# A four-layer convolution kernel: x1's last count in two parts, the last norm's factors in two parts, steps of giving out moved among x3's factors, three buffers for the normed columns

## The chip, the core and the metric

The kernel runs on one core of a Trainium2 chip. The metric is the device time of one execution in microseconds, and lower is better. A core has five engines that each work through their own queue of instructions: PE (TensorE, matrix products), DVE (VectorE), ACT (ScalarE), POOL (GpSimd) and SP (SyncE, which here only issues transfers). "PEld" is PE's loading of weights.

## What is computed

Four layers follow each other, each added to its input after a group norm over groups of four channels. The tensor has 4 images of 128 x 128 places with 128 channels.

```
x = x + relu(deform_conv(gn(x)))          # layer 0, bilinear samples at learned offsets
x = x + scan(gn(x), W)                    # layer 1, row y uses row y-1 through a 9-tap conv
x = x + z_self + z_m + z_k                # layer 2, sums over rows and columns
x = x + triangle(gn(x))                   # layer 3:
    xn = layer_norm(x); left, right = xn@left_w * sigmoid(..), xn@right_w * sigmoid(..)
    out = einsum('bkjd,bkid->bijd', left, right)
    out = (layer_norm(out) * out_gate) @ to_out_w
```

`gn` needs the mean and the variance of a whole image before any of it can be normed; in the last layer the layer norm of `out` needs them for each of its columns of 128 channels.

## The kernel before

All engines run in the order in which the program emits their instructions (`tc.manual_schedule`); generators with `yield` interleave the streams by hand, and a `step(...)` advances one of them.

**Layer 0** (`deform_layer`, lines 189 to 774) goes through blocks of three rows. Finished rows go into chunks of 16 rows (`x1c`, L576), are stored to DRAM (L586), and DVE counts each chunk, group by group (`bn_stats`, L590), into `stats`, which holds 8 chunks. When an image is done, `gn_steps` (L153) aggregates the eight counts of each of 32 groups (`bn_aggr`, L158), averages over partitions with two small matmuls (L165, L177) and ends in `scale_shift` (L92 to L96). For the last image this happens after the last convolution (L755 to L760). Then `far` is worked out: whether an offset was over 1 (L764 to L773). All engines load `far`, and jump over a general form of the layer where it is 0 (L1725).

**Layer 1** (`scan_layer`, L1011) loads rows of x1 (L1055), turns them (L1064), norms them on ACT (L1068) and runs the recurrence (L1101 to L1142), with PE nearly always busy.

**Layers 2 and 3** (`last_layers`, L1286) go image by image (L1663 to L1701). For an image b: `messages` (L1338) makes layer 2's result and counts it; `scaled` (L1389) turns the counts into factors of x3 (aggregation L1393, small matmuls L1396, L1407, L1419, square root L1409, reciprocal L1410); `normed` (L1463) centres and norms in 25 steps; `multiplied` (L1513) makes left, right and their products in four quarters of 24 steps. Between them, one step at a time, runs `given_out(b - 1)` (L1563), which norms the products of the image before, gates, multiplies by `to_out_w`, adds x3 and stores. The last image's giving out runs alone at the end (L1702); the code calls that `alone`.

One giving out has 40 steps, k from -7 to 32. Step k stores block k-1 (L1604), loads x3 for block k+2 (L1607), turns the normed columns of block k+1 on PE (L1612), makes y on ACT (L1614) and gates it (L1615, on POOL, or on DVE if alone), multiplies block k (L1623, L1627), counts block k+7 (L1578), norms the columns of block k+2 into `u` (ACT L1642, POOL L1640), evicts block k (L1644) and loads gates (L1649). In every fourth step `scales` (L1580) makes the factors for a group of four blocks from their counts: four small DVE operations (L1589 to L1592), a square root on ACT (L1595), a reciprocal and a product on DVE (L1596, L1597). They are first used by `u` two steps later. `u` has two buffers. ACT needs another table for the square root than for the sigmoids of `multiplied`, and loads it in between.

Of the kernel before, what the change touches and what calls it, by code (L numbers as in the profile page):

```python
# [10 lines left out]
F32 = mybir.dt.float32  # L11
# [3 lines left out]
ALU = mybir.AluOpType  # L15
# [4 lines left out]
P = 128  # L20
B = 4
S = 128
# [4 lines left out]
GS = 4  # L27
NGN = P // GS
# [121 lines left out]
    return (mean, *scale_shift(nc, c, keep, mean, var, tag))  # L150


def gn_steps(nc, c, work, keep, psum, stats, tag, got):  # L153

    n = stats.shape[2]
    mv = work.tile([P, NGN, 2], F32, name="gf_mv")
    for g in range(NGN):
        nc.vector.bn_aggr(mv[:, g, :], stats[:, g, :, :].rearrange("p n s -> p (n s)", n=n))  # L158
        if g % 8 == 7:
            yield  # L160
    mean_bc = psum.tile([P, NGN], F32, name="gn_ps", tag="gn_ps")
    mcol = work.tile([P, NGN], F32, name="gf_mcol")
    nc.vector.tensor_copy(mcol, mv[:, :, 0])
    yield
    nc.tensor.matmul(mean_bc, lhsT=c.mean, rhs=mcol, start=True, stop=True)  # L165
    yield
    d = work.tile([P, NGN], F32, name="gf_d")
    nc.vector.tensor_tensor(d, mcol, mean_bc, ALU.subtract)
    nc.vector.tensor_tensor(d, d, d, ALU.mult)
    nc.vector.tensor_tensor(d, d, mv[:, :, 1], ALU.add)  # L170
    wide = work.tile([P, 2, NGN, GS], F32, name="gf_wide")
    nc.vector.tensor_copy(wide[:, 0], mcol.unsqueeze(2).to_broadcast([P, NGN, GS]))
    nc.vector.tensor_copy(wide[:, 1], d.unsqueeze(2).to_broadcast([P, NGN, GS]))
    yield
    col = psum.tile([P, 2], F32, name="gn_ps2", tag="gn_ps")
    for i in range(2):
        nc.tensor.matmul(  # L177
            col[:, i : i + 1], lhsT=wide[:, i].rearrange("p g r -> p (g r)"),
            rhs=c.mean[:, 0:1], start=True, stop=True,
        )  # L180
    yield
    mvp = work.tile([P, 2], F32, name="gf_mvp")
    nc.vector.tensor_copy(mvp, col)
    yield
    got.extend(scale_shift(nc, c, keep, mvp[:, 0:1], mvp[:, 1:2], tag))
    yield


def deform_layer(tc, c, small, x, w_off, b_off, w_def, x1, tabs, offs):
# [11 lines left out]
    nc = tc.nc  # L201
# [6 lines left out]
    with ExitStack() as ctx:  # L208
        wp = ctx.enter_context(tc.tile_pool(name="l0w", bufs=1))
        keep = ctx.enter_context(tc.tile_pool(name="l0keep", bufs=2))  # L210
        one = ctx.enter_context(tc.tile_pool(name="l0one", bufs=1))
        two = ctx.enter_context(tc.tile_pool(name="l0two", bufs=2))
        three = ctx.enter_context(tc.tile_pool(name="l0three", bufs=3))
# [73 lines left out]
        last = moving("parts_of_last", 2, 1)  # L287
# [300 lines left out]
        def count(n):  # L588
            for _ in range(min(n, len(to_count))):
                nc.vector.bn_stats(*to_count.pop(0))  # L590
# [40 lines left out]
        ready = [0] * B  # L631
        beside = {"now": None, "norms": [], "rows": 0, "count": iter(())}

        def x1_norm(b, stats):
            got = []
            yield from gn_steps(nc, c, one, small, ps_g, stats, f"x1_{b}", got)
            norms[b] = got[1:]

        def counting(b):
# [74 lines left out]
        for n, (b, j) in enumerate(blocks):  # L714
# [29 lines left out]
            else:  # L744
# [7 lines left out]
                        stats, NU // 2,  # L752
                    ),
                )
        for _ in convs:  # L755
            pass
        count(len(to_count))
        beside["norms"].append(x1_norm(B - 1, stats))
        while step():
            pass  # L760

# [9 lines left out]
        nc.vector.tensor_scalar(row, row, 1.0, None, ALU.is_gt)  # L771
        far = small.tile([1, 1], I32, name="far")
        nc.vector.tensor_copy(far, row)  # L773
        return norms, far


# [509 lines left out]
def last_layers(tc, c, terms, w, x2T, out, x3T, gateT, stdT):  # L1286
# [9 lines left out]
    with ExitStack() as ctx:  # L1296
# [20 lines left out]
        def single(shape=(P, 512)):  # L1317
            return ps_s.tile(list(shape), F32, name="one_ps", tag="one_ps")
# [70 lines left out]
        def scaled(b):  # L1389

            stats = xs.pop(b)
            mv = two.tile([P, 2], F32, name="mv3")
            nc.vector.bn_aggr(mv, stats.rearrange("p n s -> p (n s)"))  # L1393
            nc.vector.tensor_tensor(mv[:, 0:1], mv[:, 0:1], w.outb, ALU.subtract)
            mean_ps = single((P, 1))
            nc.tensor.matmul(mean_ps, lhsT=c.gmean, rhs=mv[:, 0:1], start=True, stop=True)  # L1396
            mean = two.tile([P, 1], F32, name="mean3")
            nc.vector.tensor_copy(mean, mean_ps)
            d = two.tile([P, 1], F32, name="d3")
            nc.vector.tensor_tensor(d, mv[:, 0:1], mean, ALU.subtract)  # L1400
            nc.vector.tensor_tensor(d, d, d, ALU.mult)
            nc.vector.tensor_tensor(d, d, mv[:, 1:2], ALU.add)
            for j0 in range(S // 2 if b else 0, S, 16):
                nc.scalar.dma_start(x3T[b, :, j0 : j0 + 16, :], X[:, j0 : j0 + 16, :])
            yield
            var_ps = single((P, 1))
            nc.tensor.matmul(var_ps, lhsT=c.gmean, rhs=d, start=True, stop=True)  # L1407
            s = two.tile([P, 1], F32, name="s3")
            nc.scalar.activation(s, var_ps, AF.Sqrt, bias=c.eps)  # L1409
            nc.vector.reciprocal(s, s)  # L1410
            cs = one.tile([P, P], F32, name="cs")
            nc.vector.tensor_scalar(cs, c.center, s, None, ALU.mult)

            shift = two.tile([P, 1], F32, name="shift")
            nc.vector.tensor_tensor(shift, mean, w.outb, ALU.add)
            nc.vector.scalar_tensor_tensor(shift, shift, -1.0, s, ALU.mult, ALU.mult)
            yield
            pc = single((P, 1))
            nc.tensor.matmul(pc, lhsT=c.center, rhs=shift, start=True, stop=True)  # L1419
            ct = two.tile([P, 1], F32, name="ct")  # L1420
            nc.vector.tensor_copy(ct, pc)
            to_one = two.tile([P, 1], F32, name="to_one")
            nc.vector.tensor_copy(to_one, ct)
            nc.vector.memset(to_one[0:1], 1.0)
            xs[b] = cs, ct, to_one
            yield
# [136 lines left out]
        def given_out(b):  # L1563
# [6 lines left out]
            if alone:  # L1570
                groups.update({1: 0, 4: 1})
            st, factors, us, ys, gates, x3s, outs = {}, {}, {}, {}, {}, {}, {}

            def statistics(k):
                if k % 4 == 0:
# [4 lines left out]
            def scales(k0, k1):  # L1580

                n = 4 * (k1 - k0)
                both = two.tile([P, n, 2], F32, name="both", tag=f"both{n}")
                apart = two.tile([P, n], F32, name="apart", tag=f"apart{n}")
                rs = two.tile([P, n], F32, name="rs", tag=f"rs{n}")
                nm = two.tile([P, n], F32, name="nm", tag=f"nm{n}")

                s = st[k0 // 4][:, k0 % 4 * 4 : k0 % 4 * 4 + n]
                nc.vector.tensor_tensor(both, s[:, :, 1:3], s[:, :, 4:6], ALU.add)  # L1589
                nc.vector.tensor_tensor(apart, s[:, :, 1], s[:, :, 4], ALU.subtract)  # L1590
                nc.vector.tensor_tensor(apart, apart, apart, ALU.mult)
                nc.vector.scalar_tensor_tensor(  # L1592
                    rs, apart, P / 4.0, both[:, :, 1], ALU.mult, ALU.add
                )
                nc.scalar.activation(rs, rs, AF.Sqrt, bias=c.eps, scale=1.0 / P)  # L1595
                nc.vector.reciprocal(rs, rs)  # L1596
                nc.vector.scalar_tensor_tensor(nm, both[:, :, 0], -0.5, rs, ALU.mult, ALU.mult)  # L1597
                for k in range(k0, k1):
                    at = [slice(i, i + 1) for i in range(4 * (k - k0), 4 * (k - k0) + 4)]
                    factors[k] = [(rs[:, i], nm[:, i]) for i in at]  # L1600

            for k in range(-7, NS_ + 1):
                if 0 <= k - 1:
# [25 lines left out]
                        )  # L1629
                if k + 7 < NS_:  # L1630
                    statistics(k + 7)
                    if k + 8 in groups:
                        scales(groups[k + 8], k + 8)
                if 0 <= k + 2 < NS_:
                    u = us[k + 2] = two.tile([P, 4, P], F32, name="u")
                    for j, (r, m) in enumerate(factors.pop(k + 2)):
                        of = column(b, 4 * (k + 2) + j)
                        to = u[:, j].rearrange("p (q d) -> p q d", q=NQ)
                        if j >= (1 if alone else 2):
                            nc.gpsimd.tensor_scalar(to, of, r, m, ALU.mult, ALU.add)  # L1640
                        else:
                            nc.scalar.activation(to, of, AF.Identity, bias=m, scale=r)  # L1642
                if 0 <= k < NS_:
                    nc.scalar.copy(x3, po)  # L1644
                    outs[k] = x3
                k += 3 if alone else 2
                if 0 <= k < NS_:
                    gates[k] = three.tile([P, 4, S], F32, name="gate")
# [8 lines left out]
        def step(of, n=1):  # L1657
            return all([next(of, END) is not END for _ in range(n)])
# [4 lines left out]
        for b in range(B):  # L1663

            for n, _ in enumerate(msgs):
                if n % 2:
                    step(out_of)
            for _ in scaled(b):
                pass
            norm = normed(b)  # L1670
            for n in range(25):
                step(norm)
# [114 lines left out]
```

## Time and profile before

| what | value |
|---|---|
| time, median of 3 runs | 5434.85 us (5428.95 to 5440.65) |
| the profiled execution's own time | 5449.07 us |
| its span, first to last instruction | 5447.3 us |
| mean granted clock of PE | 0.957 |

| stretch (us) | what runs | PE busy (us) | DVE busy (us) | ACT busy (us) | PE clock |
|---|---|---|---|---|---|
| 0 to 3050 | layer 0 | 2752.57 | 1844.85 | 1463.35 | 0.96 |
| 3050 to 3068 | its last convolution | 17.35 | 0.92 | 0.00 | 0.69 |
| 3068 to 3098 | x1's last norm, the jump, first rows | 2.25 | 16.92 | 0.29 | 0.50 |
| 3098 to 3958 | scan | 853.32 | 582.34 | 259.90 | 0.99 |
| 4027 to 4311 | layer 3, image 0 | 248.97 | 167.36 | 100.22 | 0.96 |
| 4311 to 4666 | image 1, image 0 given out | 312.13 | 214.08 | 181.08 | 0.95 |
| 4666 to 5020 | image 2, image 1 given out | 309.98 | 213.74 | 181.28 | 0.96 |
| 5020 to 5329 | image 3, image 2 given out | 280.62 | 161.33 | 180.91 | 0.96 |
| 5329 to 5448 | image 3 given out, alone | 81.47 | 74.94 | 62.27 | 0.77 |

In lines of a group or of the timeline, "out<-in" names the tiles; what stands in brackets or after the bar is the engine's idle time just before, and what ended it. A line of the waits says who waited for whom, in total, how often, and the longest.

### The profile page before, as it was taken

To read this page: it belongs to the slowest core of one execution; us is meant where nothing else is said; L and a number is where in the kernel's file an instruction comes from. 1 tells how busy PE (TensorE), PEld (TensorE's weight loads), DVE (VectorE), ACT (ScalarE), POOL (GpSimd) and SP (SyncE) were. 2 spreads that over 40 slices of the span, in tenths; PEclk is the share of its full clock that TensorE was granted. 3 is DMA by queue.
4 is the path that set the end of the run, shared out by engine and by line. 5 is a ranking of instruction groups with operands and counts; after the bars stand their busy time and mean duration, and the time that the engine had idled before them with its cause. 6 is when DMAs were issued, how large, how long until landed. Compare 5 with 4: busy or idle time off the path is not lost. (4 is left out here: it accounts for less than half of the span.)

```text
span 5447.3 us, 162742 instructions
## 1 busy us (share of the span) xinstructions
PE 4898.7 (90%) x68902; PEld 4254.0 (78%) x68902; DVE 3333.0 (61%) x8447; ACT 2431.9 (45%) x5045; POOL 1233.1 (23%) x1145
## 2 busy tenths in 40 slices
PE   1898999999999898989999799999969889798897
PEld 1787788888888787877899799999928578485686
DVE  4676666666566666665555466666664765756645
ACT  1554454544554444545544223333324364463655
POOL 4222121210221201212100011111120342422424
PEclk9999999999998999999999899999989999999997
DMA  5776656675666665665644322222242554645535
GB/s 151 160 159 150 138 135 141 147 151 102 137 142 132 150 121 110 147 132 119 132 83 89 85 82 78 78 78 78 67 142 92 174 182 130 212 144 170 187 113 194
DMA packets 1357657, 710.41 MB, mean 130 GB/s; under 512 B 943885, under 2 KB 1210414, under 8 KB 1347702
## 3 DMA queue, kind: packets, MB, share of 16 engines
q1 hardware_dynamic: 1322770, 624.74, 47.0%
q10 hardware_dynamic: 34148, 75.15, 3.7%
q8 instruction: 545, 8.93, 0.7%
q14 instruction: 194, 1.59, 0.1%
HBM read 417.02 MB, written 282.55 MB: 128 GB/s over the span
## 5 line engine op out<-in xcount | busy, mean ns | idle before, releaser
L606 PE MATMUL conv_ps<-ring,wdef 128*128 128x192 f32 (+2 forms) x7632 | 1301.6, 320 | 7.1 <-DVE x1c L576 5.7
L514 DVE TENSOR_TENSOR m<-t_ps,tent 128x390 f32<-128x390 f32 x1548 | 806.2, 557 | 788.7 <-ACT tent L512 772.8
L606 PEld LDWEIGHTS conv_ps<-ring,wdef 128*128 128x128 f32 x7632 | 1147.6, 196 | 127.6 <-issue 64.0
L512 ACT COPY tent<-t_ps 128x390 f32<-128x390 f32 x1560 | 691.1, 488 | 659.7 <-PE t_ps L498 648.3
L498 PE MATMUL t_ps<-parts_of,spread 57*64 57x99 bf16 (+1 forms) x12384 | 743.6, 275 | 168.1 <-DVE m L514 146.4
L523 PE MATMUL v_ps<-m,pixels 60*64 60x108 f32 (+1 forms) x22704 | 813.4, 264 | 20.3 <-DVE m L514 8.7
L498 PEld LDWEIGHTS <-spread 57*64 57x64 bf16 x12480 | 579.3, 126 | 312.1 <-issue 265.1
L523 PEld LDWEIGHTS v_ps<-m,pixels 60*64 60x64 f32 x22704 | 673.5, 137 | 70.5 <-DVE m L514 21.7
L549 ACT COPY ring<-v_ps 128x432 f32<-128x432 f32 x1032 | 505.7, 525 | 445.3 <-PE v_ps L523 444.7
L1526 PEld LDWEIGHTS pair_ps<-wcat,X 128*128 128x128 f32 x4096 | 491.0, 196 | 118.3 <-issue 75.3
L420 POOL TENSOR_TENSOR off<-off,koff 72x512 f32<-72x512 f32 x128 | 162.8, 1272 | 1772.7 <-DVE off L417 1772.7
L1526 PE MATMUL pair_ps<-wcat,X 128*128 128x128 f32 x4096 | 505.4, 281 | 57.4 <-DVE X L1461 36.1
L1534 DVE TENSOR_TENSOR T<-pair_ps,sig 128x256 f32<-128x256 f32 x512 | 281.4, 592 | 366.0 <-ACT sig L1531 365.4
L1112 PEld LDWEIGHTS own_ps<-diff,wconv 128*128 128x128 f32 x4064 | 494.8, 191 | 13.3
L1112 PE MATMUL own_ps<-diff,wconv 128*128 128x128 f32 x4064 | 495.6, 273 | 0.0
L506 PE MATMUL t_ps<-parts_of,spread 57*64 57x130 bf16 x9288 | 455.5, 225 | 0.0
L1152 POOL TENSOR_TENSOR sum_h<-sum_h,x2c 128x512 f32<-128x512 f32 x128 | 163.2, 1275 | 1147.3 <-DVE x2c L1138 689.8
L438 DVE SCALAR_TENSOR_TENSOR parts<-off,parts 72x512 bf16<-72x512 f32 x384 | 296.3, 772 | 152.2 <-ACT parts L430 146.5
L1068 ACT ACTIVATE rowT<-x1T_ps,t_x,s_x 128x128 f32<-128x128 f32 x512 | 207.2, 567 | 310.2 <-PE x1T_ps L1064 307.6
L506 PEld LDWEIGHTS <-spread 57*64 57x64 bf16 x9312 | 320.0, 108 | 0.1
L1531 ACT ACTIVATE sig<-pair_ps 128x512 f32<-128x512 f32 x256 | 152.4, 597 | 365.0 <-PE pair_ps L1526 264.3
L1101 PE MATMUL both_ps<-carry,wsum 128*128 128x128 f32 x2032 | 269.2, 274 | 1.1 <-DVE carry L1135 1.1
(200 smaller groups left out, 6681.0 us busy)
## 6 DMA issues: line engine op xcount, KB each, us to landing
pixels<-tab SPq DMA_DIRECT2D x688, 123.8 KB
parts_of<-off SPq DMA_DIRECT2D x1032, 55.7 KB
off<-parts SPq DMA_DIRECT2D x64, 891.0 KB
tab<-rows SPq DMA_DIRECT2D x384, 128.0 KB
xin<-in_x_dram SPq DMA_DIRECT2D x128, 256.0 KB
x<-x1c SPq DMA_DIRECT2D x32, 1024.0 KB
x1rows<-x SPq DMA_DIRECT2D x128, 256.0 KB
x2T<-x2c ACTq DMA_DIRECT2D x128, 256.0 KB
```

The costliest lines, as they stand in the source:

```text
L438: nc.vector.scalar_tensor_tensor(parts[:, NSPLIT + i, h : h + RO, 2 : S + 2], off, 0.0, part, ALU.is_gt, ALU.mult,)
L498: nc.tensor.matmul(tp[h : h + HALF, 0, 0:n].rearrange("p (r c) -> p r c", c=PADW)[:, :, i:PADW:RX], lhsT=spread[0:k, kx // 2, i, h : h + H ...
L506: nc.tensor.matmul(tp[h : h + HALF, 1, i * PADW : (i + 1) * PADW], lhsT=spread[HALF : HALF + k, kx // 2, first + i, h : h + HALF], rhs=src ...
L512: nc.scalar.copy(tent[:, 0:n], tp[:, 0, 0:n])
L514: nc.vector.tensor_tensor(m, *pair, ALU.mult)
L523: nc.tensor.matmul(to[p1 : p1 + HALF], lhsT=pix[p0 : p0 + LANES, xb, :], rhs=m[p0 : p0 + LANES, :, RX * xb : RX * xb + w], start=True, sto ...
L549: nc.scalar.copy(to, bodies[side])
L606: nc.tensor.matmul(pc[:, at : at + rows, x0:x1], lhsT=wdef[:, side, k, :], rhs=v[:, :, k if v.shape[2] == NK else kx, x0 + kx : x1 + kx], ...
L1101: nc.tensor.matmul(both, lhsT=wsum[:, j, :], rhs=old[h][:, 1, :, j : j + V], start=(j == 0), stop=(j == NJ - 1),)
L1112: nc.tensor.matmul(own[:, n], lhsT=wt[:, 2 * j + n, :], rhs=diffs[h][:, n, :, j : j + V], start=False, stop=(n == 1 and j == NJ - 1),)
L1526: nc.tensor.matmul(pj[:, j], lhsT=X[:, j0 + j, :], rhs=w.wcat[:, q * 4 * DQ : (q + 1) * 4 * DQ], start=True, stop=True,)
L1534: nc.vector.tensor_tensor(to, pj[:, :, e].rearrange("p j d -> p d j"), sig[:, :, e].rearrange("p j d -> p d j"), ALU.mult,)
```

## The change

Four edits:

1. `gn_steps` takes `apart`. With it, it aggregates only the first 7 of 8 counts of each group, and joins the eighth by ten operations on 128 x 32 (128 x 64) elements. For the last image, 8 of the 32 aggregations are emitted after each of four parts of the last convolution, then the last chunk is counted and joined. `far` is worked out before that convolution.
2. `scales` is a generator in three parts: DVE's four operations in the step in which it was, the square root, the reciprocal and the product at the end of the next step. The factors are so made one step later, and used in the step after.
3. `u` has three buffers.
4. `scaled` has one more `yield`, after L1394, and at its first two yields a step of giving out is made. There are no more steps than before: each step from the third on comes two places earlier, and the last two places, in the last quarter of `multiplied`, are empty.

```diff
-def gn_steps(nc, c, work, keep, psum, stats, tag, got):
+def gn_steps(nc, c, work, keep, psum, stats, tag, got, apart=False):
-    n = stats.shape[2]
+    n = stats.shape[2] - apart
     mv = work.tile([P, NGN, 2], F32, name="gf_mv")
     for g in range(NGN):
-        nc.vector.bn_aggr(mv[:, g, :], stats[:, g, :, :].rearrange("p n s -> p (n s)", n=n))
+        nc.vector.bn_aggr(mv[:, g, :], stats[:, g, 0:n, :].rearrange("p n s -> p (n s)", n=n))
         if g % 8 == 7:
             yield
+    if apart:
+        h, last = S // (n + 1) * GS / 2.0, stats[:, :, n, :]
+        both = work.tile([P, NGN, 2], F32, name="gf_both")
+        off = work.tile([P, NGN], F32, name="gf_off")
+        nc.vector.tensor_tensor(both, last[:, :, 1:3], last[:, :, 4:6], ALU.add)
+        nc.vector.tensor_tensor(off, last[:, :, 1], last[:, :, 4], ALU.subtract)
+        nc.vector.tensor_tensor(off, off, off, ALU.mult)
...
+        nc.vector.scalar_tensor_tensor(
+            mv[:, :, 1], both[:, :, 1], 1.0 / (2 * h * (n + 1)), off, ALU.mult, ALU.add
+        )
...
-        for _ in convs:
-            pass
-        count(len(to_count))
-        beside["norms"].append(x1_norm(B - 1, stats))
         while step():
             pass
...
         nc.vector.tensor_copy(far, row)
+        count(len(to_count))
+        last_norm = x1_norm(B - 1, stats, True)
+        for _ in convs:
+            next(last_norm)
+        count(len(to_count))
+        for _ in last_norm:
+            pass
         return norms, far
...
             nc.vector.tensor_tensor(mv[:, 0:1], mv[:, 0:1], w.outb, ALU.subtract)
+            yield
             mean_ps = single((P, 1))
...
+            scaling = []
...
             def scales(k0, k1):
...
                 nc.vector.scalar_tensor_tensor(
                     rs, apart, P / 4.0, both[:, :, 1], ALU.mult, ALU.add
                 )
+                yield
                 nc.scalar.activation(rs, rs, AF.Sqrt, bias=c.eps, scale=1.0 / P)
...
                     factors[k] = [(rs[:, i], nm[:, i]) for i in at]
+                yield
...
                 if k + 7 < NS_:
                     statistics(k + 7)
-                    if k + 8 in groups:
-                        scales(groups[k + 8], k + 8)
                 if 0 <= k + 2 < NS_:
-                    u = us[k + 2] = two.tile([P, 4, P], F32, name="u")
+                    u = us[k + 2] = three.tile([P, 4, P], F32, name="u")
...
                     nc.scalar.copy(x3, po)
                     outs[k] = x3
+                for part in scaling:
+                    next(part)
+                scaling.clear()
+                if k + 8 in groups:
+                    part = scales(groups[k + 8], k + 8)
+                    next(part)
+                    scaling.append(part)
...
-            for _ in scaled(b):
-                pass
+            for n, _ in enumerate(scaled(b)):
+                if n < 2:
+                    step(out_of)
```

## The prediction

> **What bounds the kernel now.** I read the page first, then the busy times by stretch, then the waits and the timeline of the three places that the diff touches. The page gives TensorE most of the span:
>
> ```profile
> span 5447.3 us, 162742 instructions
> PE 4898.7 (90%) x68902; PEld 4254.0 (78%) x68902; DVE 3333.0 (61%) x8447; ACT 2431.9 (45%) x5045; POOL 1233.1 (23%) x1145
> ```
>
> So an edit pays only where TensorE stands still. First place, between layer 0 and the scan (timeline):
>
> ```profile
> 3068.16 0.29 DVE L576 SCALAR_TENSOR_TENSOR x1c<-conv_ps,xres 128x128 f32<-128x128 f32 x1 [6.82 <-PE conv_ps L606]
> ...
> 3068.48 4.15 DVE L590 BATCH_NORM_STATS2 stats<-x1c 128x6 f32<-128x64 f32 x32
> 3072.56 7.48 DVE L158 BATCH_NORM_AGGREGATE gf_mv<-stats 128x2 f32<-128x48 f32 x32
> 3080.08 0.18 DVE L163 COPY gf_mcol<-gf_mv 128x32 f32<-128x32 f32 x1
> ...
> 3083.59 0.21 DVE L96 TENSOR_SCALAR t_x<-gf_mvp,s_x 128x1 f32<-128x1 f32 x1
> ...
> 3085.00 0.14 DVE L773 CAST far<-most_row 1x1 int32<-1x1 f32 x1
> ```
>
> Columns: start, duration. VectorE alone works from 3068.2 to 3085.1; then every engine loads `far`, jumps (PE's compare-and-branch at L1725 takes 3829 ns) and the first x1 rows are fetched at 3092.85, after all engines have raised their semaphores behind the jump (VectorE at 3089.9).
>
> Second place, the last giving out (5328 to the end), waits of PE and of ACT (total, times, longest):
>
> ```profile
> PE one_ps L1612 <- ACT u L1642: 31.2, 9, 8.1
> ```
> ```profile
> ACT rs L1595 <- DVE rs L1592: 25.6, 9, 4.4
> ACT x L1644 <- PE one_ps L1627: 15.0, 15, 1.4
> ```
> One of those stops in the timeline:
> ```profile
> 5383.76 0.17 DVE L1592 SCALAR_TENSOR_TENSOR rs<-apart,both 128x16 f32<-128x16 f32 x1
> 5383.97 0.31 ACT L1595 ACTIVATE rs<-rs,eps 128x16 f32<-128x16 f32 x1 [2.95 <-DVE rs L1592]
> 5384.18 0.58 ACT L1642 ACTIVATE u<-T,nm,rs 128x128 f32<-128x128 f32 x1
> ...
> 5384.82 1.11 PE L1612 MATMUL one_ps<-ident,u 128*128 128x128 f32 x4 [3.29 <-ACT u L1642]
> ```
>
> ScalarE's square root stands ahead of `u` in its queue and waits for a count that VectorE has just reached; `u` needs nothing from it, and TensorE waits for `u`. It recurs every 13.7 us (5370.5, 5384.2, 5397.9). Third place, the same stop in images 1 to 3, beside other work (window 4310 to 4665):
>
> ```profile
> PE pair_ps L1526 <- DVE X L1461: 8.9, 7, 5.6
> ...
> PE pair_ps L1526 <- DVE T L1534: 7.1, 6, 3.0
> ...
> PE one_ps L1612 <- ACT u L1642: 5.5, 8, 1.8
> ```
> ```profile
> ACT rs L1595 <- DVE rs L1592: 18.0, 7, 3.9
> ```
>
> **What the skill says.** "TensorE: Matmul & The Clock Gate", Part 1 (the HAM clock gate): idle time in a window of some 3.4 us halves the clock. The trace agrees: the clock is 0.77 in the last 119 us, and after the stop above four transposes take 1.11 us, not 0.60. "Runtime: NRT & Kernel Launch", Instruction fetch mechanics: a taken branch to far code waits for a fetch; here 3.8 us, as above. "ScalarE: Activation LUTs", What ACT_TABLE_LOAD costs: 1283 ns; the trace has 1283, but no extra drain after it. "SBUF — State Buffer", the shared port pair: a VectorE operation with two SBUF inputs locks GpSimd out; in the last stage the y product takes 691 to 977 ns, and three `u` on POOL 2.09 us instead of 1.66 alone.
>
> **Part 1, the last count.** Twenty-four of 32 aggregations move ahead of the last eviction or beside the last convolution (VectorE idles 9.65 and 6.82 us before the two evictions); instruction order leaves 8 behind it. `far` moves ahead of the last convolution. Step by step: `most`'s matmul now stands before the conv matmuls and waits for two copies and a reduction: copy ends 3051.12, reduction 0.27, matmul 0.40, so PE restarts about 3051.9 instead of 3050.65: +1.2. After the last eviction: 8 x 0.23 = 1.85 instead of 7.48 (-5.6). Added: 10 small operations on 128x32, spaced like L168 to L170 at 0.22: +2.2. Sum at the factors: -2.2. Then 1.4 of `far` (3083.72 to 3085.14) leaves the chain: the DVE jump ends 3.6 earlier, 3086.3. SP, whose `far` load now stands before its last store, has jumped long before, and so has not the 2.9 us that it now spends between the last semaphore (3089.9) and its first fetch (3092.85); I take -2.7 of it. Together -6.3. Bounds: 0, if the 10 operations cost double and PE's own jump ends last; -9.
>
> **Part 2, two steps of giving out inside `scaled`.** For b = 1 to 3 those are steps k = -5 and -4, which hold no matmul: they put four counts (1.20) ahead of the copy of the mean, which waits 0.74 for PE now (+0.45), and four counts and four small operations (1.2 + 0.8 = 2.0) ahead of L1410, which waits 1.03 now (+0.97). So +1.4 an image on a path on which PE is idle: +4.2. All later steps come two places earlier: two full steps (about 2.0 of PE each) enter the norm phase, as much leaves the last two quarters, whose cost a step is the same (q1 is 15.8 longer with 7 steps than in image 0). Their loads of x3 and gates and the stores on SP move with them, past two or three stdT transfers; x3 has four buffers, and the extra DMA falls in a phase at 0.43 share: nothing, or +0.5 an image without that cover.
>
> **Part 3, factors in two parts, images 1 to 3.** VectorE's part stays in step k; square root, reciprocal and nm go to the end of step k+1. ScalarE then never waits for the count. Table loads stay as many. New wait: the reciprocal waits behind y, u and x3 in ScalarE's queue; behind it on VectorE are X or T, which need a later ScalarE result anyway: nothing. Gains, image 1: in the norm phase PE stops of 0.74, 1.08 and 1.25 before L1612, I take -2.5; in the first quarter the 5.57 stop holds ScalarE's wait of 3.05: -3.0 (two table loads stay); the stops of 2.98 and 2.60 in later quarters, I take -2.0. Sum -7.5, bounds 0 and -11 (all gaps and the slow clock behind them). Three images: -22.5. With part 2: -18.3.
>
> **Part 4, the same in the last giving out.** VectorE has 2.07 a step (L1615 and four L1578, 5393.55 to 5395.62), 1.3 more a group: 4 x 2.07 + 1.3 = 9.6 for four steps against 13.7. But nm comes a step later, and the group's first `u` has one step of slack, not two. From the start of y in a step with a count at 0: count and four operations to 2.87; next y and counts to 4.95; reciprocal and nm to 5.45; POOL's three `u` 2.1, so 7.6. PE is free at 5.25 and stands 2.35; transposes to 8.2, y on ScalarE to 9.0, VectorE's y at 9.1 instead of 7.5. Cycle 11.2; if the stop halves the clock for 3.4 us, 12.9. Stops of 2.0 have done so (5344.9), one of 2.6 not (4525.2); I take two in three, 12.3. Seven cycles x 1.4 = -10. The ring of three lets POOL start `u` without waiting for L1612 (34.0 us of POOL waits): it serves this and has no price of its own. Bounds: -28.7 (9.6) and +17.5 (below).
>
> **Sum.** -6.3 - 18.3 - 10 = -34.6. The profiled execution is 5449.1 (span 5447.3 and 1.8 around it), so about 5414.5; it stands 14.2 above the median of 5434.85, so 5400.
>
> **Rivals.** (a) Everything hides: POOL is ahead, VectorE alone bounds the end (-28.7), images give -11 each, +4.2: -6.3 - 28.7 - 28.8 = -64, 5371. For: VectorE's sum; against: the late nm. (b) The stop only moves: cycle 12.9 (-5.6), images keep their PE idle time (+4.2), part 1 bounded by PE's jump (-3): about 5430. For: PE 57 of 63 us busy in the norm phase, so little to gain. That the count's split does nothing is in this case. (c) Slower: late factors. The group's first transposes stop 2.35 in each cycle and keep the clock at half: four steps of 3.45 and the stop make 16.2, +2.5 x 7 = +17.5; images gain nothing, +4.2; with part 1's -6.3: 5450. It decides from where the stop leaves no full window busy; against it, clock recovers within 6.8 us after 3.3 us stops now.
>
> **Chances.** Forecast (5385 to 5418) 0.68, (a) 0.12, (b) 0.13, (c) 0.07. A measurement of this kernel can tell about 0.2% (10.9 us) from no change. Faster 0.80 (forecast and a), same 0.13, slower 0.07. The range reaches to (a) and (b), 5372 to 5430.
>
> **What would show it.** Right: no ScalarE wait of L1595's line for VectorE; L1612 stops of about 2.3 us, one a group, ended by POOL; first x1 rows fetch about 6 us sooner after the last eviction; L1410's wait gone in `scaled` and 1.4 longer chain. Wrong: last stage not under 115 us, images 1 and 2 still at 354 us, or a stop of PE ahead of the conv matmuls over 2 us.

## The result and the profile after

| | before | after |
|---|---|---|
| median (us) | 5437.75 of 4 runs (5428.95 to 5447.36) | 5380.59 of 4 runs (5363.54 to 5384.22) |
| the profiled execution's own time (us) | 5449.07 | 5377.80 |
| its span (us) | 5447.3 | 5376.1 |
| mean granted clock of PE | 0.957 | 0.966 |

The ratio is 0.9888, with a 95% interval of 0.9861 to 0.9916. The kernel is 57 us faster, where 34.6 were forecast. The time of 5380.6 lies below the forecast's own band (5385 to 5418) and inside its whole range (5372 to 5430). The head of the page after:

```profile
span 5376.1 us, 162726 instructions
PE 4866.8 (91%) x68902; PEld 4222.0 (79%) x68902; DVE 3328.1 (62%) x8457; ACT 2435.3 (45%) x5045; POOL 1229.1 (23%) x1145
```

PE does the same 68902 matmuls. Its busy time falls by 31.9 us while its mean clock rises, and VectorE has ten instructions more. The lines have moved: L158 is now L159, L1526 L1558, L1592 to L1597 are L1625 to L1631, L1612 L1647, L1642 L1675.

First place, after layer 0, from the timeline (start, duration):

```profile
3061.51 0.29 DVE L602 SCALAR_TENSOR_TENSOR x1c<-conv_ps,xres 128x128 f32<-128x128 f32 x1 [1.03 <-PE conv_ps L632]
3061.72 1.75 DVE L159 BATCH_NORM_AGGREGATE gf_mv<-stats 128x2 f32<-128x42 f32 x8
3063.39 4.09 DVE L616 BATCH_NORM_STATS2 stats<-x1c 128x6 f32<-128x64 f32 x32
3067.52 0.26 DVE L167 TENSOR_TENSOR gf_both<-stats 128x64 f32<-128x64 f32 x1
...
3069.62 0.17 DVE L189 COPY gf_mcol<-gf_mv 128x32 f32<-128x32 f32 x1
...
3073.12 0.21 DVE L96 TENSOR_SCALAR t_x<-gf_mvp,s_x 128x1 f32<-128x1 f32 x1
...
3077.28 12.48 SPq L1086 DMA_DIRECT2D x1rows<-x  x12
...
3082.90 2.64 PE L1095 MATMUL x1T_ps<-ident,x1rows 128*128 128x128 f32 x9 [10.53 <-DMA gcol<-in_norm_g_dram]
```

From the last eviction's end to the copy of the means it is 7.8 us, and was 11.6. Eight aggregations are left behind it, and the ten joining operations follow each other at 0.22 us. The fetch of the first rows and the first turned row ended this stretch before, too:

```profile
3092.85 11.73 SPq L1055 DMA_DIRECT2D x1rows<-x  x12
...
3097.91 3.26 PE L1064 MATMUL x1T_ps<-ident,x1rows 128*128 128x128 f32 x12 [13.38 <-DMA x1rows<-x]
```

From the last eviction's end to the first turned row it is 21.1 us, and was 29.5.

Second place, the last giving out, waits (total, times, longest):

```profile
...
PE one_ps L1658 <- DMA x<-x3T: 18.9, 17, 2.3
...
PE one_ps L1647 <- ACT u L1675: 9.5, 3, 7.7
...
ACT rs L1629 <- DVE rs L1625: 4.6, 2, 4.0
...
PE one_ps L1647 <- POOL u L1673: 2.1, 10, 0.2
```

ScalarE's wait ahead of the root went from 25.6 us to 4.6, and PE's wait for `u` behind it from 31.2 to 9.5, of which 7.7 is the start. The forecast's new stop, PE waiting 2.35 us a group for GpSimd's `u`, is not there: ten waits of 0.2 at most. Instead PE waits for x3, 17 times. Why x3 is late stands in SyncE's queue of the same stretch:

```profile
SPq L1642 <- DMA out_dram<-x: 34.2, 27, 3.2
```

x3's tile is also the tile that is stored. It has four buffers, so the load for block k+2 (L1642) waits for the store of block k-2 to land. In the kernel before, SyncE waited 2.0 us for such stores in this stretch.

Third place, image 1, PE's waits (4297 to 4615):

```profile
...
PE pair_ps L1558 <- DVE X L1493: 5.9, 6, 1.8
PE one_ps L1647 <- POOL u L1673: 4.0, 5, 2.8
PE pair_ps L1558 <- DVE T L1566: 2.9, 5, 1.4
...
PE one_ps L1647 <- ACT u L1675: 1.2, 4, 0.6
```

L1526's waits for X and T were 8.9 and 7.1, the longest 5.6; L1612's for ScalarE's `u` were 5.5. One wait grew: for GpSimd's `u` from 2.2 us (longest 1.2) to 4.0 (longest 2.8). In the six profiles with edits 2 and 4 the longest such wait of an image is 2.0 to 3.2 us, and 1.2 in the four with neither.

The two profiles can't be subtracted as a whole. Layer 0 up to its last sampling product, which no edit touches, ends between 3035.4 and 3058.1 us in the profiles of this study. So I compare stretches, and take each from several profiles that share its code.

### The profile page after: what moved, and what is told of

The parts are those of the page before. It is cut to its first block, busy times and chain, and to the rows that moved or that the text cites. A ratio compares the mean times of both kernels' runs of the same rounds, so it can differ in the third digit from the quotient of the medians.

```text
span 5376.1 us, 162726 instructions
## 1 busy us (share of the span) xinstructions
PE 4866.8 (91%) x68902; PEld 4222.0 (79%) x68902; DVE 3328.1 (62%) x8457; ACT 2435.3 (45%) x5045; POOL 1229.1 (23%) x1145
## 5 line engine op out<-in xcount | busy, mean ns | idle before, releaser
L1558 PEld LDWEIGHTS pair_ps<-wcat,X 128*128 128x128 f32 x4096 | 480.3, 193 | 95.6 <-issue 70.3
L1558 PE MATMUL pair_ps<-wcat,X 128*128 128x128 f32 x4096 | 493.4, 277 | 34.6 <-DVE X L1493 24.7
L1566 DVE TENSOR_TENSOR T<-pair_ps,sig 128x256 f32<-128x256 f32 x512 | 281.6, 592 | 318.3 <-ACT sig L1563 317.4
```

What stands on the lines that cost most here:

```text
L1558: nc.tensor.matmul(pj[:, j], lhsT=X[:, j0 + j, :], rhs=w.wcat[:, q * 4 * DQ : (q + 1) * 4 * DQ], start=True, stop=True,)
L1566: nc.vector.tensor_tensor(to, pj[:, :, e].rearrange("p j d -> p d j"), sig[:, :, e].rearrange("p j d -> p d j"), ALU.mult,)
```

## The experiments

All ratios are against the kernel before, from the runs of the same chip; totals in us are differences of medians.

**Each edit alone.** The first four kernels add one of the four edits, as numbered in the section on the change, to the kernel before; their diffs are the parts of the diff there.

Edit 1 alone:

```diff
-        for _ in convs:
-            pass
-        count(len(to_count))
-        beside["norms"].append(x1_norm(B - 1, stats))
...
+        last_norm = x1_norm(B - 1, stats, True)
+        for _ in convs:
+            next(last_norm)
```

> The kernel before with edit 1 alone (the last count in two parts). Theory from the trace of the whole change: the stretch from the last sampling product of layer 0 to the first turned row of x1 takes about 37 us instead of 47, all of it between VectorE's last eviction and the first row; total -8 to -11 us. Rival, the forecast's sum: -6.3 us, with PE stopped 1.2 us ahead of the last convolution. Images 1 to 3 and the last giving out as in the kernel before.

Measured: ratio 0.9985 (0.9973 to 0.9996), 5430.43 beside 5439.08, so -8.7. The interval is 12 us wide, and so the total can't tell the theory's -8 to -11 from the rival's -6.3. The stretches can say more. From the last eviction to the first turned row it is 21.1 us; four profiles without any of edit 1 have 29.35 to 29.94, so -8.4. Of PE's stop ahead of the convolution, which the rival had, the timeline of the changed kernel shows 0.65 us and a short matmul:

```profile
3043.85 1.97 PE L549 MATMUL v_ps<-me,pixels 60*64 60x12 f32 x46
3046.47 0.40 PE L788 MATMUL most_ps<-ident,most 72*1 72x72 f32 x2 [0.65 <-DVE most L786]
3046.80 4.53 PE L632 MATMUL conv_ps<-ring,wdef 128*128 128x192 f32 x14
```

The product before ends at 3045.82, so this costs 1.0 us. Together that is -7.4, between theory and rival. The stretch from that product to the last eviction is 14.1 to 17.7 us without it and 15.5 to 18.8 with it, by how much of it ran at half clock.

Edit 2 alone:

```diff
+                yield
                 nc.scalar.activation(rs, rs, AF.Sqrt, bias=c.eps, scale=1.0 / P)
...
+                for part in scaling:
+                    next(part)
+                scaling.clear()
```

> The kernel before with edit 2 alone (square root, reciprocal and product one step later), u in two buffers, no steps in `scaled`. Theory from the trace of the whole change: this edit holds nearly all of what the images and the end gained: first quarter -5, second -3, third -5 in each of images 1 to 3 (together -40 us), last giving out about 104 instead of 119 us; total about -50. Rival 1, the forecast's sum: -7.5 an image and -10 at the end, -32.5. Rival 2, the ring is needed: with two buffers u waits for PE's transposes, PE stops once a group for POOL's u, the end stays above 112 us and the total is about -30.

Measured: 0.9909 (0.9887 to 0.9932), 5388.70, so -50 (-61 to -37 by the interval). This edit holds most of the gain, and needs no ring: the last giving out takes 101.95 us. But the third quarter gave only 1.2 us (57.82 to 56.62 in image 1), not 5.

Edit 3 alone:

```diff
-                    u = us[k + 2] = two.tile([P, 4, P], F32, name="u")
+                    u = us[k + 2] = three.tile([P, 4, P], F32, name="u")
```

> The kernel before with edit 3 alone (u in three buffers). Theory: within 2 us of the kernel before, as what holds u back is ScalarE's wait ahead of it and not its buffer. Rival: POOL's waits for the buffer (34 us in the last giving out) count, the last giving out gets 5 us shorter or more.

Measured: 0.9992 (0.9978 to 1.0005), 5434.35: no change that can be told. Its last giving out took 113.47 us against 118.72, which by the expectation would have been the rival's. It isn't: three other kernels with the old code there and two buffers took 110.30, 112.14 and 109.41. The 118.72 was the odd one.

Edit 4 alone:

```diff
-            for _ in scaled(b):
-                pass
+            for n, _ in enumerate(scaled(b)):
+                if n < 2:
+                    step(out_of)
```

> The kernel before with edit 4 alone (two steps of giving out inside `scaled`). Theory: `scaled` is 1 us longer in each of images 1 to 3, the quarters move by less than 2 us each in either direction as the same steps fall elsewhere; total +1 to +5. The forecast had +4.2. Rival: the moved steps bring the third quarter's and the fourth's gain of the whole change (-5 and -1 an image); total -10 or less.

Measured: 0.9980 (0.9969 to 0.9991), 5430.08, so -9.0. Here my forecast fell: `scaled` is 2.0 us longer an image, as it now holds a whole `scales`, and the norm 3.1, but the third quarter is 5.0 shorter (57.82 to 52.81 in image 1) and the fourth 2.1. (The norm is taken from the first centring matmul to the end of the last one, as the mean of images 1 to 3; the first quarter also gets 1.7 longer in images 1 and 2.) The third quarter's gain is this edit's. Its windows (stretch, length, busy time and instructions of PE, PEld, DVE, ACT, POOL, clock, DMA share, GB/s) and PE's waits, in image 1, kernel before:

```profile
4514.58:4572.40 57.82, 55.22 (x451) 50.88 (x450) 20.68 (x42) 35.71 (x61) 17.22 (x20) 1.00 0.36 119
```
```profile
PE pair_ps L1526 <- DVE T L1534: 2.6, 1, 2.6
```

Edit 2 alone:

```profile
4494.90:4551.52 56.62, 55.22 (x451) 51.04 (x450) 20.66 (x42) 35.70 (x61) 17.16 (x20) 1.00 0.35 121
```
```profile
PE pair_ps L1526 <- DVE T L1534: 1.4, 1, 1.4
```

Edit 4 alone:

```profile
4504.13:4556.94 52.81, 52.81 (x431) 48.79 (x430) 17.64 (x32) 30.54 (x52) 14.39 (x15) 1.00 0.31 110
```

Before, one square root stands in this quarter, with PE stopped for 2.6 us. ScalarE's groups say what the stop is made of (busy, mean ns, then idle before):

```profile
...
L1595 ACT ACT_TABLE_LOAD x1 | 1.3, 1283 | 0.0
L1531 ACT ACT_TABLE_LOAD x1 | 1.3, 1283 | 0.0
L1595 ACT ACTIVATE rs<-rs,eps 128x16 f32<-128x16 f32 x1 | 0.3, 308 | 1.2 <-DVE rs L1592 1.2
```

Edit 2 takes away the wait of 1.2 and leaves the two table loads, and 1.4 us of stop with them. Edit 4 moves the last group's counts and root (step 24) out of this quarter. One table load stays at its start, behind 1.5 us in which ScalarE waits for PE. PE then never stops in it, and has 2.41 us less to do, because two nearly empty last steps stand where two full ones were: 2.6 + 2.4 = 5.0.

**`far` early, the count in one part.** Only the order around `far` changes:

```diff
-        for _ in convs:
-            pass
-        count(len(to_count))
-        beside["norms"].append(x1_norm(B - 1, stats))
         while step():
             pass
...
         nc.vector.tensor_copy(far, row)
+        for _ in convs:
+            pass
+        count(len(to_count))
+        beside["norms"].append(x1_norm(B - 1, stats))
+        while step():
+            pass
```

> The kernel before with `far` worked out ahead of the last convolution, the count in one part. From the last eviction to the first turned row of x1: 29.5 us in the kernel before, 21.1 with all of edit 1. Theory: `far` takes its 1.4 us of VectorE and SyncE's 2.5 us before its first fetch with it, so 25 to 26 us. Rival: SyncE's delay follows VectorE's jump and stays, so 28 us, and the count's split holds the other 7.

Measured: 24.8 us from the last eviction to the first row, 4.7 less than before. So `far`'s place is worth 4.7 and the count's split 3.7. The theory holds within 0.2 us (25 to 26), the rival's 28 doesn't. The theory's two parts are not the whole, as VectorE's jump got shorter too (last section). With PE's stop ahead of the convolution taken off, 3.7 us are left for the total. Its ratio is 0.9999 (0.9987 to 1.0011), an interval of 13 us, too wide to show them.

**The changed kernel again, with two buffers for `u`, and with more for x3.**

> The changed kernel once more, beside those below. Theory, the sum of the four edits alone (-8 for the count, -50 for the factors, -4 for the ring, -10 for the steps) is -72 us, more than the -57 that the whole change showed; what overlaps is in the last giving out, where the changed kernel is bounded by x3's loads: ratio 0.988 to 0.990. Rival: the runs of the result were slow ones by chance and the edits add up: ratio 0.986 to 0.9875.

Measured: 0.9880 (0.9862 to 0.9899), 5380.89 beside 5442.48, so -61.6. The ratio is the theory's, but its interval reaches over the rival's range, and the sum of -72 is itself uncertain by some 17 us (an estimate from the four intervals). So an overlap isn't shown. The stretches in the table below speak against one: edits 1, 2 and 4 alone give -7.4, -42.1 and -4.8 there, together -54.3, and the whole -58.8. Last giving out 102.70.

```diff
-                    u = us[k + 2] = three.tile([P, 4, P], F32, name="u")
+                    u = us[k + 2] = two.tile([P, 4, P], F32, name="u")
```

> The changed kernel with u in two buffers again. Theory: u is not held by its buffer once ScalarE no longer waits for the counts; within 3 us of the changed kernel, last giving out 102 to 106 us. Rival, the forecast's (the ring lets GpSimd start u early and serves the late factors): a stop of PE for GpSimd's u of 1 us or more in each group of four blocks, last giving out 108 us or more, +5 us or more.

Measured: 0.9883 (0.9866 to 0.9900), 5377.76; last giving out 101.11, PE's waits for GpSimd's `u` 2.8 us in 14. So the ring brings nothing, with the factors late or not.

This profile shows one thing more. PE waits for x3 3.8 us in it, where the two profiles of the changed kernel have 18.9 and 12.5, and four of its six groups of four steps take 10.6 to 10.7 us with x3 still in four buffers. With edit 2 alone, also with two buffers for `u`, PE waits 9.6 us for x3. So four buffers for x3 don't always make it late. Whether the third buffer for `u` does is not shown: the last giving out is only 1.6 to 3.0 us shorter here, and the totals are alike.

```diff
-                    x3 = x3s[k + 2] = four.tile([P, 4, S], F32, name="x3")
+                    x3 = x3s[k + 2] = four.tile(
+                        [P, 4, S], F32, name="x3", tag="wide" if alone and k % 2 else "x3"
+                    )
```

> The changed kernel with x3 of odd blocks in another four buffers (those of `wide`, not used by then) in the last giving out. Theory: PE's waits for x3 (18.9 us, 17 times) come from x3's buffer, which is free only when the store of the block four earlier has landed; with eight buffers they fall below 4 us and the last giving out to 94 to 98 us, total -6 to -10. Rival 1: the DMA engines themselves are full (share 0.84), x3 or the gates stay late and the last giving out stays above 101. Rival 2: the stop that the forecast put there (2.35 us a group of PE for GpSimd's u, behind the late nm) takes its place: the last giving out is 98 to 102 and PE's waits for GpSimd's u exceed 10 us.

Measured: 0.9864 (0.9846 to 0.9881), 5371.79, 9 less than the changed kernel beside it; last giving out 97.89, so that this stretch shows 4.8 of the 9. Its waits (lines from L1644 on stand two later than in the changed kernel, so L1647 is now L1649):

```profile
...
PE one_ps L1649 <- ACT u L1677: 13.1, 8, 7.7
...
ACT u L1677 <- DVE nm L1631: 6.1, 5, 1.2
...
PE one_ps L1649 <- POOL u L1675: 3.1, 15, 0.2
...
PE one_ps L1660 <- DMA x<-x3T: 1.2, 3, 0.5
```

x3's wait is gone. With it out of the way the late factors show, though not as PE's 2.35 us for GpSimd. One group in the timeline:

```profile
5324.15 1.05 DVE L1652 TENSOR_TENSOR y<-y,gate 128x512 f32<-128x512 f32 x1
...
5329.32 0.17 DVE L1631 SCALAR_TENSOR_TENSOR nm<-both,rs 128x16 f32<-128x16 f32 x1
...
5329.62 0.61 ACT L1677 ACTIVATE u<-T,nm,rs 128x128 f32<-128x128 f32 x1 [1.23 <-DVE nm L1631]
5329.70 7.16 POOL L1675 TENSOR_SCALAR u<-T,rs,nm 128x128 f32<-128x128 f32 x11 [2.95 <-PE one_ps L1664]
...
5330.28 0.64 PE L1649 MATMUL one_ps<-ident,u 128*128 128x128 f32 x2 [0.74 <-ACT u L1677]
...
5331.12 0.33 PE L1649 MATMUL one_ps<-ident,u 128*128 128x128 f32 x1 [0.21 <-POOL u L1675]
...
5331.65 0.33 PE L1649 MATMUL one_ps<-ident,u 128*128 128x128 f32 x1 [0.20 <-POOL u L1675]
```

nm ends 5.3 us after the y of the step with the counts began (5324.15; the forecast had 5.45), and GpSimd's three columns take 2 us from there. But PE turns each column as it comes: it stands 0.74, 0.21 and 0.20 us, 1.15 in all and never long, and the clock stays full. (With two buffers for `u` one such group, with 0.39 more for x3, was followed by 3.4 us at half clock and took 12.4.)

**Without the steps in `scaled`.** The changed kernel with the two lines of edit 4 taken back:

```diff
-            for n, _ in enumerate(scaled(b)):
-                if n < 2:
-                    step(out_of)
+            for _ in scaled(b):
+                pass
```

> The changed kernel without edit 4 (no step of giving out inside `scaled`). Theory from the edits alone (factors alone -9.7 us an image, all four -13.9): edit 4 is worth about -4 us an image where the factors come in two parts; each of images 1 to 3 gets 3.5 to 4.5 longer: `scaled` -1, norm -2, first quarter +2, third +3.8, fourth +1.3; total +10 to +13 against the changed kernel. Rival: it is worth what it brings alone, -1.6 an image, total +5. The forecast's price, +1.4 an image, would make this kernel 4 us shorter.

Measured: 0.9916 (0.9889 to 0.9942), 5395.56, some 15 above the changed kernel (5380.89), with intervals of nearly 30 and 20 us; the totals can't tell the theory's 10 to 13 from the rival's 5. From `scaled` to the end of the fourth quarter, images 1 and 2 take 321.4 us with edit 2 and not 4 (two kernels), 330.4 with edit 4 alone, 332.0 with neither (four kernels) and 318.3 with both (six kernels). So edit 4 is worth 1.6 us an image alone and 3.1 with the factors in two parts, between the rival's 1.6 and the theory's 4. Of the 1.5 between them, `scaled` explains 1.0, as it then holds only VectorE's half of `scales` (+1.0, not +2.0). The forecast's +1.4 is out.

**Earlier factors in the last giving out.** From block 6 on, counts one step earlier; first with x3 in four buffers, then in eight:

```diff
+                ahead = 8 if alone and k >= -1 else 7
+                if alone and k == -1:
+                    statistics(6)
-                if k + 7 < NS_:
-                    statistics(k + 7)
+                if k + ahead < NS_:
+                    statistics(k + ahead)
...
-                if k + 8 in groups:
-                    part = scales(groups[k + 8], k + 8)
+                if k + ahead + 1 in groups:
+                    part = scales(groups[k + ahead + 1], k + ahead + 1)
```

> The changed kernel with the counts, and so the factors, one step earlier in the last giving out from block 6 on; x3 in four buffers. Theory: four steps of the last giving out take 11.1 us for x3's loads, so the earlier factors bring under 2 us; ScalarE's wait for nm (1.2 us a group) goes. Rival: late factors hold the cycle, it falls to about 10 and the last giving out gets 6 us shorter or more.

Measured: 0.9887 (0.9863 to 0.9911), 5380.37; last giving out 102.74, as in the changed kernel. PE waits 23.2 us for x3. The theory holds: earlier factors alone bring the changed kernel nothing that shows, while PE waits for x3; only with x3 in more buffers can they.

> As `early`, with x3 in eight buffers in the last giving out. With those alone four steps took 10.70 us, of which VectorE's own work is 9.6, and ScalarE waited 1.2 us a group for nm. Theory: late factors are the next limit; four steps take 9.6 to 9.9 us, the last giving out 91 to 93 us, 5 to 7 shorter than with eight buffers alone; total about -14 against the changed kernel. Rival 1: DMA is full, the gates come late and the cycle stays at 10.5 or more. Rival 2: PE's clock falls to half as PE waits oftener, no gain.

Measured: 0.9868 (0.9846 to 0.9890), 5370.90. Last giving out 91.86, 6.0 less than with eight buffers alone, as the theory had it. The total does not show these 6 us: it is that of the kernel with eight buffers, within intervals of 20 us. PE waits for x3 again in it, 9.5 us in 12 waits, though SyncE waits for no store before these loads. The transfers fill more of the time, in this window of the last giving out:

```profile
5300.00:5374.00 74.00, 62.16 (x490) 54.55 (x489) 60.19 (x167) 55.77 (x97) 57.06 (x85) 1.00 0.91 310
```

The changed kernel moves 268 GB/s at a share of 0.85 there. Whether full DMA engines or SyncE's queue (its stores wait 25.1 us for ScalarE's eviction, ahead of the loads) make x3 late now was not tested. The two kernels with eight buffers have the lowest medians of the study, but their intervals overlap that of the changed kernel.

## Why the prediction was right, and where its sum was off

The sign and the three places were right, the sum 23 us short: one term had the wrong sign and one was too small. In the table, part 1 is from edit 1's profiles, parts 2 and 3 from images 1 and 2 above, times three, and part 4 from five profiles each of old and new code. Its sum lies near the two measured totals, -57 and -61.6.

| step of the forecast | forecast (us) | measured (us) |
|---|---|---|
| part 1, last count and `far` | -6.3 | -8.4 + 1.0 = -7.4 |
| part 2, steps in `scaled` | +4.2 | -4.8 alone, -9.3 in the whole |
| part 3, factors, images 1 to 3 | -22.5 | -31.9 |
| part 4, last giving out | -10 | -10.2 (112.8 to 102.6) |
| sum | -34.6 | -58.8 |

**Part 1** was near in each term that it priced: the count 3.4 forecast (5.6 less 2.2) and 3.7 measured, `far` 4.1 (1.4 and 2.7) and 4.7, PE's stop 1.2 and 1.0. In the changed kernel SyncE's first fetch (3077.28) is issued 0.5 us after VectorE's arrival behind the jump (3076.80); 2.9 us lay between them before. Two terms were not priced and partly cancel: VectorE's jump takes 1.3 us less, and from the first fetch to the first turned row it takes 0.6 us more.

**Part 2** failed in its sign. The failing step is "two full steps (about 2.0 of PE each) enter the norm phase, as much leaves the last two quarters, whose cost a step is the same". The entering half was right (+3.1 in the norm). But a mean cost a step doesn't hold for the last steps of a generator: steps from 25 on have no counts, and step 24 has the last square root with its two table loads. Listing which k fell into which quarter would have shown that the third quarter loses the only root that it had. The price in `scaled`, 1.4, was measured as 1.0 in the whole and 2.0 alone.

**Part 3** had the right mechanism and a term too small. The norm gave 2.0 (forecast 2.5) and the first quarter 4.0 (3.0), as means of images 1 to 3. For "the stops of 2.98 and 2.60 in later quarters, I take -2.0" the runs show 2.3 in the second quarter and 1.2 in the third of image 1. The stop of 2.60 would have been priced well by its own rows: 1.2 is ScalarE's wait, which goes, and the rest stays with the table loads. The rest of the 10.6 is 0.6 of clock in the third quarter and 0.5 spread over other stretches: in four profiles of the old code five of twelve third quarters take 59.3 to 59.5 us and the others 57.8, and with edit 2 all take 56.6. The forecast's bound of -11 held. Its "New wait: ... nothing" did not: PE's longest wait for GpSimd's `u` in an image is 2.5 to 2.7 us with edit 2 alone, and was 1.2. The gains above are net of it.

**Part 4** was right in size through two errors that cancelled. The cycle of 13.7 us, read from the profile, is not the usual one. Five profiles of the same code have means of 11.9 to 13.5 for the first six groups, 12.45 over all. In the profile before, half clock and full clock take turns of 6.8 us each from 5349.7 to 5431.6, so that one turn of both is as long as one group; the other four show this in three groups at most. The windows in the kernel before and in edit 1 alone differ in the clock (0.77, 0.92):

```profile
5344.76:5440.00 95.24, 73.64 (x468) 70.56 (x468) 60.86 (x162) 55.73 (x96) 58.17 (x84) 0.77 0.73 234
```
```profile
5318.55:5405.00 86.45, 65.16 (x474) 59.77 (x475) 58.98 (x163) 56.27 (x96) 57.70 (x84) 0.92 0.79 262
```

The new cycle of 12.3 was 11.0 (five profiles of new code). The forecast let the stop halve the clock in two of three cases; it is full from 5287 us on in the changed kernel and from 5295 with eight buffers for x3. With edit 2 alone and with two buffers for `u`, it is half once, for 3.4 us, in a group of 12.9 and of 12.4 us, near the forecast's 12.9 for that case. Its undisturbed cycle of 11.2, late nm and all, is near what eight buffers show: 10.7. That PE would stand 2.35 us for GpSimd was wrong, as columns come one by one. That the sum of this part came out at -10 is luck. What is late next after the root's stop is x3's load, which the forecast named only as hidden ("x3 has four buffers").

**The rivals.** (a), everything hides, came nearest in time with 5371, but not by its mechanism: part 4 gave 10 us and not 28.7. Its bounds for part 1 and for the images were nearly met, and part 2 gave most of what it lacked. (b) is out, since PE's idle time in the images went. (c), the late factors, is out: PE's stops for them are 1.15 us in a group and not 2.35, the clock stays full, and earlier factors alone changed nothing.

What stays open: edit 4 brings 1.5 us an image more in the whole than alone. One is `scaled`; the other half microsecond is not told apart from the clock. Whether the earlier factors lower the total beyond eight buffers wasn't settled, nor what makes x3 late with four buffers in some profiles and hardly in one.

## What to carry to other kernels

Before you move steps of a generator, write down which steps fall into each stretch and what each issues. The last ones and every fourth one are not the mean one: a square root with its table loads that left a full stretch was worth 2.6 us here (1.4 with its wait gone already), beside 2.4 for the matmuls that left with it.

A wait on an in-order engine and the table loads around it are separate prices: splitting the step takes away the first only. And once a wait is removed, ask for the buffer that is next: a tile that is loaded, overwritten and stored is free only when its store has landed.

If a stretch's clock is low in one profile, price it from several profiles of the same code before you call its cycle the usual one.

## What the runs showed of the hardware

- The same code of the last giving out took 109.4 to 118.7 us in five profiles, with a granted clock that differs from one to the next. The Trainium skill, "TensorE: Matmul & The Clock Gate", Part 1 (the HAM clock gate), says that the clock is halved after an idle window of some 3.4 us, and that the window which is watched runs freely, so that it depends on where in it the work falls. The profiles agree with the second: with stops of about 3 us in both the clock is 0.77 in the kernel before and 0.92 with edit 1 alone, in the windows above.
- In all thirteen profiles the granted clock changes only on a fixed grid of 3.41 us, within 0.01 us. Here the measurement differs from the page: a window of this grid need not be idle throughout to cost the clock. Counted over all profiles, half clock followed every one of the 428 windows at full clock in which PE was idle for 60% or more, and 75 of 17295 in which it was idle for less than 35%; full clock came back only after windows idle for less than 20% (the ends of matmuls are modelled). So the place of a stop counts. With edit 2 alone one of 1.81 us, up to 5346.07, fell into one window and halved the clock; in the second profile of the changed kernel one of 2.58 us, up to 5346.32, was shared by two windows, and the clock stayed full. The columns are those of edit 4's windows, with the clock third from the end:

```profile
5342.98:5346.39 3.41, 1.59 (x13) 1.22 (x13) 2.51 (x9) 2.42 (x5) 1.81 (x3) 1.00 0.85 252
5346.39:5349.81 3.42, 3.42 (x18) 3.42 (x18) 2.15 (x7) 1.14 (x3) 0.00 (x0) 0.50 0.85 298
```
```profile
5341.59:5345.00 3.41, 1.96 (x16) 1.75 (x16) 2.52 (x7) 2.43 (x5) 2.79 (x5) 1.00 0.76 207
5345.00:5348.42 3.42, 2.08 (x17) 1.91 (x18) 2.20 (x10) 0.63 (x3) 0.00 (x0) 1.00 1.00 353
5348.42:5351.83 3.41, 2.67 (x16) 1.76 (x16) 2.54 (x9) 2.02 (x5) 2.47 (x4) 1.00 0.92 275
```

- In this last stage the 16 DMA engines moved 310 GB/s at a busy share of 0.91 with eight buffers for x3 and early factors, and 268 at 0.85 in the changed kernel, where SyncE waited for stores to land.
- VectorE's load and jump between its last operation and its arrival behind the jump took 4.8 us in the kernel before (3085.1 to 3089.9) and 3.3 us with only `far` moved (3079.67 to 3082.99), though the code behind is the same. It is 4.6 to 4.8 us in all four profiles with `far` late, and 3.3 to 3.5 in all nine with `far` early. Why isn't shown.
